# Weaving one image's way back with the next image's way forward in a spectral convolution layer

## The chip, the cores and the metric

The kernel runs on one core of a Trainium2 chip. The metric is device time in microseconds for one launch, the median of several runs. The profile is one execution, taken by the hardware profiler.

## The reference

Two layers on x of shape (4, 192, 128, 128), float32, each with a residual and a group normalisation (32 groups) ahead of it. Layer 0, the one that the change concerns, does this for each image:

```python
x1 = c1x1(gn(x), conv1_w)                      # 192 -> 48 channels
x_0, x_05, x_1 = x1[:, :16], x1[:, 16:32], x1[:, 32:48]
Fre = frft2d(x_05, 0.5)                        # fractional Fourier transform, 2-D
mag, pha = abs(Fre), angle(Fre)
mag_out = c1x1(c3x3(mag * mask1) * mask1 + c1x1(mag * mask2) * mask2)
pha_out = c1x1(pha)
ifrft = abs(frft2d(mag_out * exp(1j * pha_out), -0.5))
fre = rfft2(x_1)
mo, po = c1x1(abs(fre)), c1x1(angle(fre))
x_1o = irfft2(mo * exp(1j * po))
x = x + c1x1(concat([c1x1(x_0), ifrft, x_1o]), conv2_w)    # 48 -> 192 channels
```

Layer 1 is a selective state space scan over the 16384 positions of each image (384 inner channels, 16 states). It takes most of the time and isn't touched.

## The kernel before

Layer 0 treats the four images b = 0..3 in turn, with four kinds of work, each a Python generator. Its `yield`s mark the places at which another generator's instructions may be put in between. Program order is only the first input: the tile framework's scheduler may move an instruction ahead of others on its engine, inserts all semaphores and holds a tile's next writer until its last reader is done. Each engine, and SP's queue of DMA issues, then works through its own fixed order.

- `analysis(b)`: reads the image in 16 pieces of 8 rows (`load`, L196), takes statistics of each on DVE (`bn`, L202), finishes the group statistics (`bn_done`, L209 and L56 to L67), scales the weights of the first 1x1 convolution, and reads the pieces again (the last four, `KEEP`, are kept) for that convolution on PE (L292). ACT adds the bias (L296) and stores the result to the DRAM tensor `d1` from its own queue (L302). 33 steps: 16 pieces, then 16 pieces more, and the end.
- `branches(b)`, its first part, the way forward: reads 32 channels of d1 as `img` (L308). `spectrum` applies the two-sided transforms as matmuls with constant matrices (L224, L234), ACT and DVE copy real and imaginary part out (L240, L242), and `_polar` makes magnitude and phase: Square, Abs, Sqrt and Arctan on ACT (L76 to L90), an addition on POOL (L78), and twelve operations on DVE (L84 to L96), of which the reciprocal at L87 is the longest. This is done in three portions: two halves of the fractional branch, whose results SP stores to `dmag` and `dp` (L317), and the Fourier branch, stored to `dh` (L324).
- `branches(b)`, its second part, the way back: reads magnitude (`magQ`, L330 to L336) and phase (L353) in another layout, does the masked 3x3 convolution (L362) and the 1x1 convolutions (L254) in four steps, and `_from_polar` (L109 to L118) makes real and imaginary part, stored to `df` (L386). The Fourier branch follows in the same way from `dh` (L397) to `di` (L406). Then the inverse transforms: eight steps of L421 and L429 with ACT between, reading df (L414); four of L451 and L459, reading di (L442). The result goes to the DRAM tensor `dimg` (L467).
- `synthesis(b)`: for each of 16 pieces, reads the piece of x again (L196) and the channels of d1 and dimg into `cat` (L479, L480), does the last 1x1 convolution (L485), adds it to x on DVE (L489), takes statistics for layer 1 (L202) and stores to `xmid` from POOL's queue (L493). 16 steps and the end.

The order is written out by hand. analysis(0) runs alone. Then, for each image, branches(b) sets the beat: at each of its steps, one or two steps of analysis(b+1) and of synthesis(b-1) are taken, and what is left of these follows. For the last image, synthesis(2) starts from step `HOLD` = 10, and at step `LOADS` = 18 four pieces for synthesis(3) are read ahead. synthesis(3) runs alone.

Pools: image pieces `xt` have 7 buffers, polar temporaries `u` (128 x 1040 float32) 10, shared by the ways forward and back, `img` 2, and the temporaries of the convolutions and inverse transforms 2 each. PSUM has four single banks `ps` for all kinds of work and two double banks `pr`. Layer 1 opens its pools when those of layer 0 are closed.

Of the kernel before, what the change touches and what calls it, by code (L numbers as in the profile page):

```python
# [22 lines left out]
NC = 16  # L23
# [79 lines left out]
def _from_polar(nc, pool, half_pi, mag, pha, n):  # L103

    def tmp():
        return pool.tile([128, NC * L], F32, name="u")[:, 0:n]

    k, co = tmp(), tmp()
    nc.vector.tensor_scalar(k, pha, 1.0 / (2.0 * math.pi), ROUND, ALU.mult, ALU.add)  # L109
    nc.vector.tensor_scalar(k, k, -ROUND, None, ALU.add)  # L110
    for part in (TWO_PI_HI, TWO_PI_MID, TWO_PI_LO):
        nc.vector.scalar_tensor_tensor(pha, k, -part, pha, ALU.mult, ALU.add)
    nc.vector.tensor_scalar(pha, pha, PI_F32, -PI_F32, ALU.min, ALU.max)
    nc.scalar.activation(co, pha, AF.Abs)
    nc.scalar.activation(co, co, AF.Sin, bias=half_pi, scale=-1.0)
    nc.scalar.activation(pha, pha, AF.Sin)
    nc.vector.tensor_mul(pha, pha, mag)
    nc.vector.tensor_mul(mag, co, mag)  # L118
    return mag, pha


def layer0(tc, x, xmid, st2, w):
# [1 line left out]
    nc = tc.nc  # L124
    B = x.shape[0]
    KEEP = 4
    HOLD = 10
    LOADS = 18
    with ExitStack() as ctx:
        def pool(name, bufs, **kw):  # L130
            return ctx.enter_context(tc.tile_pool(name=name, bufs=bufs, **kw))

        cp = pool("l0c", 1)
        dram = pool("l0d", 2, space=DRAM)
        xp = pool("l0x", 7)
        sp = pool("l0s", 2)
        imp = pool("l0i", 2)
        zp = pool("l0z", 2)
        up = pool("l0u", 10)
        qp = pool("l0q", 1)  # L140
        psA = pool("l0p", 4, space=PSUM)
        psB = pool("l0r", 2, space=PSUM)
# [159 lines left out]
                        nc.scalar.dma_start(out=at[q], in_=x1[64 * q : 64 * q + 3 * NC])  # L302
                yield

        def branches(b, got):

            xT = imp.tile([128, 2 * NC, S], F32, name="img")
            nc.sync.dma_start(out=xT, in_=got["d1"][NC:, :].rearrange("c (h w) -> h c w", h=S))  # L308

            dm = dmag[b % len(dmag)]  # L310
            dp = dram.tile([NC * S, S], F32, name="dp")
            for half in range(2):
                mag, pha = yield from spectrum(
                    xT, 0, fr2[:, 0, :], fr2, S, (2 * half, 2 * half + 1)
# [3 lines left out]
                        out=by_row(dst, 8 * half, 8), in_=src.rearrange("k (c l) -> k c l", c=8)  # L318
                    )

            dh = [dram.tile([NC * S, L], F32, name=f"dh{i}") for i in range(2)]
            polar = yield from spectrum(xT, NC, rf1, rf2, L, range(4))
            for src, dst in zip(polar, dh):
                nc.sync.dma_start(  # L324
                    out=by_row(dst, 0, NC), in_=src.rearrange("k (c l) -> k c l", c=NC)
                )


            magQ = qp.tile([128, 18, S], F32, name="magQ")
            nc.sync.dma_start(  # L330
# [16 lines left out]
            dpv = dp.rearrange("(p r) l -> p (r l)", r=16)  # L347
            for half in range(2):
                n = 8 * S
                mo = up.tile([128, NC * L], F32, name="u")[:, 0:n]  # L350
                po = up.tile([128, NC * L], F32, name="u")[:, 0:n]
                ph = up.tile([128, NC * L], F32, name="u")[:, 0:n]
                nc.sync.dma_start(out=ph, in_=dpv[:, half * n : (half + 1) * n])  # L353
                for q in range(2):
                    r0 = 8 * half + 4 * q
                    at = slice(512 * q, 512 * (q + 1))
                    psf = linear(9, magQ[:, 1 + r0 : 5 + r0, :], 512)
                    pss = psA.tile([128, 512], F32, name="ps")
                    v = pss[:, 0 : 4 * WIN].rearrange("p (r l) -> p r l", r=4)
                    for tap in range(9):  # L360
                        i, j = divmod(tap, 3)
                        nc.tensor.matmul(  # L362
                            v, bd[:, tap, :], magC[:, r0 + i : r0 + i + 4, j : j + WIN],
                            start=tap == 0, stop=tap == 8,
                        )
                    f = zp.tile([128, 4, S], F32, name="f")
                    s = zp.tile([128, 4, WIN], F32, name="s")
                    nc.scalar.activation(
                        f, psf.rearrange("p (r l) -> p r l", r=4), AF.Identity, bias=bdb[:, 1:2]
                    )  # L370
                    fc = f[:, :, LO:HI]
                    rows = slice(1 + r0, 5 + r0)
                    nc.vector.tensor_tensor(fc, fc, _bc(rm[:, 1, rows], 2, WIN), ALU.mult)
                    nc.vector.scalar_tensor_tensor(
                        s, v, bdb[:, 0:1], _bc(rm[:, 0, rows], 2, WIN), ALU.add, ALU.mult
                    )
                    nc.vector.tensor_add(fc, fc, s)
                    nc.scalar.activation(
                        mo[:, at], linear(10, f, 512), AF.Identity, bias=bdb[:, 2:3]
                    )  # L380
                    nc.scalar.activation(
                        po[:, at], linear(11, ph[:, at], 512), AF.Identity, bias=bdb[:, 3:4]
                    )
                    yield
                for src, dst in zip(_from_polar(nc, up, half_pi, mo, po, n), df):
                    nc.sync.dma_start(  # L386
                        out=dst.rearrange("(p r) l -> p (r l)", r=16)[:, half * n : (half + 1) * n],
                        in_=src,
                    )
# [3 lines left out]
            di = [dram.tile([NC * S, L], F32, name=f"di{i}") for i in range(2)]  # L393
            inner = []
            for src in dh:
                t = up.tile([128, NC * L], F32, name="u")
                nc.sync.dma_start(out=t, in_=src.rearrange("(p r) l -> p (r l)", r=16))  # L397
                for q in range(4):
                    at = slice(4 * L * q, 4 * L * (q + 1))
                    nc.scalar.activation(  # L400
                        t[:, at], linear(12, t[:, at], 4 * L), AF.Identity, bias=bdb[:, 4:5]
                    )
                inner.append(t)
                yield
            for src, dst in zip(_from_polar(nc, up, half_pi, *inner, n), di):
                nc.sync.dma_start(out=dst.rearrange("(p r) l -> p (r l)", r=16), in_=src)  # L406


            img = imp.tile([128, 2 * NC, S], F32, name="img")
            for half in range(2):  # L410
                fq = [up.tile([128, NC * L], F32, name="u")[:, 0 : 8 * S] for _ in range(2)]
                fq = [t.rearrange("k (c l) -> k c l", c=8) for t in fq]
                for t, src in zip(fq, df):
                    nc.sync.dma_start(out=t, in_=by_row(src, 8 * half, 8))  # L414
                for q in range(4):
                    z = zp.tile([128, 2, 2, S], F32, name="zi")
                    ps = psA.tile([128, 512], F32, name="ps")
                    v = ps.rearrange("p (c r l) -> p c r l", c=2, r=2)
                    for cc in range(2):
                        for r in range(2):  # L420
                            nc.tensor.matmul(  # L421
                                v[:, cc], fq[r][:, 2 * q + cc, :], fi_cat[:, r], start=r == 0, stop=r == 1
                            )
                    nc.scalar.copy(z, v)
                    ps = psA.tile([128, 512], F32, name="ps")
                    v = ps.rearrange("p (c r l) -> p c r l", c=2, r=2)
                    for cc in range(2):
                        for r in range(2):
                            nc.tensor.matmul(  # L429
                                v[:, cc], z[:, cc, r, :], fi_cat[:, r], start=r == 0, stop=r == 1  # L430
                            )
                    sq = zp.tile([128, 2, 2, S], F32, name="sq")
                    nc.scalar.activation(sq, v, AF.Square)
                    c = 8 * half + 2 * q
                    nc.gpsimd.tensor_add(img[:, c : c + 2, :], sq[:, :, 0, :], sq[:, :, 1, :])
                    yield
            nc.scalar.activation(img[:, 0:NC, :], img[:, 0:NC, :], AF.Sqrt)

            hq = [up.tile([128, NC * L], F32, name="u") for _ in range(2)]
            hq = [t.rearrange("k (c l) -> k c l", c=NC) for t in hq]  # L440
            for t, src in zip(hq, di):
                nc.sync.dma_start(out=t, in_=by_row(src, 0, NC))  # L442
# [27 lines left out]
        def synthesis(b, got, early):  # L470
# [25 lines left out]
                yield  # L496
            bn_done(st, st2[:, b])

        got = [{} for _ in range(B)]
        for _ in analysis(0, got[0]):
            pass
        behind = iter(())
        for b in range(B):
            ahead = analysis(b + 1, got[b + 1]) if b + 1 < B else iter(())
            early = []
            for i, _ in enumerate(branches(b, got[b])):
                next(ahead, None)
                if b < B - 1 or i >= HOLD:  # L510
                    next(ahead if i % 2 and b < B - 1 else behind, None)
                if b == B - 1 and i == LOADS:
                    early = [load(b, p) for p in range(KEEP)]
            for rest in (behind, ahead):
                for _ in rest:
                    pass
            behind = synthesis(b, got[b], early)
        for _ in behind:
            pass

# [696 lines left out]
```

## Time and profile before

| | |
|---|---|
| median of 3 runs | 11385.26 us (11378.39 to 11391.84) |
| the profiled execution, its own time | 11385.68 us |
| its span, from the first to the last instruction | 11383.6 us |
| mean granted TensorE clock | 0.934 |
| PE, DVE, ACT, POOL busy | 92%, 92%, 82%, 86% of the span |
| bytes moved by DMA | 1481.93 MB |

PE is TensorE, PEld its weight loads, DVE VectorE, ACT ScalarE, POOL GpSimd, SP the engine that issues most DMAs. A line number such as L317 is that of the profiled kernel before. In a table of stages each row gives a stretch of the span in us from its start, the busy us of each engine with its instruction count in brackets, the granted TensorE clock, the mean busy share of the 16 DMA engines, and the GB/s that they moved. In a list of waits "SPq L317 <- ACT u L79" says that a DMA issue of line 317 on SP's queue stood until ACT had done line 79 on tile u; the numbers are the total in us, how often, and the longest. The profile spans the whole program; layer 0 is its first 1376 us.

### The profile page before, as it was taken

Reading aid. Unit: us, or ns where it says so; the run is one execution under the profiler, and the core shown is the slowest. Engines: PE = TensorE matmul, PEld = TensorE weight load, DVE = VectorE, ACT = ScalarE, POOL = GpSimd, SP = SyncE. Lnnn points to the kernel's source line nnn. Section 1 sums busy time; section 2 is a strip of 40 time slices with the busy share of each in tenths; the row PEclk is TensorE's granted clock in tenths of the full one; section 3 lists DMA queues with packets and bytes.
Section 4 is the critical chain, followed back from the end, with each engine's and each line's share of the span. In section 5 each row is a group of like instructions: output and inputs, shape, how many; then the busy total and the mean of one; then the engine's idle time right before and its main releaser. Section 6 shows DMA issues by size and latency. Waiting matters only on the chain.

```text
span 11383.6 us, 163735 instructions
## 1 busy us (share of the span) xinstructions
PE 10442.3 (92%) x54154; PEld 7012.0 (62%) x54154; DVE 10486.9 (92%) x11073; ACT 9317.9 (82%) x17507; POOL 9813.9 (86%) x4470
## 2 busy tenths in 40 slices
PE   4777799999999999999999999999999999999998
PEld 2444366666666666666666666666666666666666
DVE  6565689999999999999999999999999999999999
ACT  2323189889889889889889889889889889889887
POOL 0000099999999999999999999999999999999999
PEclk8888799999999999999999999999999999999999
DMA  7787744344344344344344344344344344344343
GB/s 197 199 222 184 206 127 119 114 128 120 113 128 121 112 128 122 111 128 123 110 128 124 109 128 125 108 128 126 107 129 126 106 130 127 105 130 128 104 130 99
DMA packets 1339287, 1481.93 MB, mean 130 GB/s; under 512 B 903281, under 2 KB 954214, under 8 KB 1337926
## 3 DMA queue, kind: packets, MB, share of 16 engines
q1 hardware_dynamic: 1317958, 1408.54, 42.6%
q0 software_dynamic: 13312, 50.34, 1.3%
q10 hardware_dynamic: 7168, 12.59, 0.3%
q8 instruction: 429, 7.03, 0.3%
q14 instruction: 420, 3.44, 0.1%
HBM read 1312.63 MB, written 155.32 MB: 129 GB/s over the span
## 4 chain that ended last, share of the span: by engine, by line
DVE 31%; ACT 29%; PE 27%; issue 8%; DMA 3%; POOL 2%; DVEq 0%; SPq 0%; POOLq 0%; ACTq 0%
DVE h L892 21%; ACT da L822 9%; ACT dbT L866 6%; PE py L918 6%; DVE op L842 5%; PE ps L686 4%; PE ps L705 4%; PE ps L956 4%; ACT L822 3%; PE op L878 2%; ACT op L822 2%; ACT L713 1%; POOL db L850 1%; PE ps L675 1%; ACT dt L770 1%
## 5 line engine op out<-in xcount | busy, mean ns | idle before, releaser
L905 POOL TENSOR_TENSOR hc<-h,bc 128x1024 f32<-128x1024 f32 x3072 | 7188.5, 2367 | 216.5 <-PE ps L942 142.2
L892 DVE TENSOR_TENSOR_SCAN h<-da,carry,op 128x512 f32<-128x512 f32 x4216 | 5197.9, 1261 | 19.6 <-ACT da L822 6.5
L918 PEld LDWEIGHTS py<-ident,hc 128*128 128x128 f32 x24576 | 2999.3, 148 | 851.2 <-issue 698.3
L918 PE MATMUL py<-ident,hc 128*128 128x128 f32 x24576 | 3401.3, 285 | 30.6 <-ACT yt L927 16.9
L822 ACT ACTIVATE da<-dt,c_A_log 128x512 f32<-128x512 f32 x4352 | 2994.7, 724 | 187.2 <-DVE h L892 172.0
L892 DVE TENSOR_TENSOR_SCAN h<-op,carry,db 128x512 f32<-128x512 f32 x1736 | 2201.1, 1268 | 128.5 <-POOL db L850 123.9
L850 POOL TENSOR_TENSOR db<-dtu,bc 128x1024 f32<-128x1024 f32 x896 | 2143.0, 2392 | 4.8 <-DMA bc<-dbc 4.7
L842 DVE TENSOR_TENSOR op<-dp,bc 128x512 f32<-128x512 f32 x2816 | 1886.6, 670 | 11.5 <-ACT dp L805 11.5
L822 ACT ACTIVATE op<-dt,c_A_log 128x512 f32<-128x512 f32 x1792 | 1223.0, 683 | 680.8 <-DVE h L892 678.0
L866 ACT ACTIVATE dbT<-ps,bT 128x128 f32<-128x128 f32 x6144 | 1656.1, 380 | 0.0
L686 PE MATMUL ps<-s,c_wiT 96*128 96x512 f32 x3072 | 1522.3, 620 | 5.2 <-ACT xs L699 3.6
L705 PE MATMUL ps<-xs,dcw 128*128 128x512 f32 x3072 | 1424.7, 593 | 1.4 <-ACT u L713 1.4
L878 PE MATMUL op<-ident,dbT 128*128 128x128 f32 x6144 | 1077.1, 296 | 112.5 <-DVE h L892 76.8
L878 PEld LDWEIGHTS op<-ident,dbT 128*128 128x128 f32 x6144 | 780.6, 151 | 408.2 <-ACT dbT L866 208.2
L686 PEld LDWEIGHTS ps<-s,c_wiT 96*128 96x128 f32 x3072 | 557.8, 199 | 469.6 <-issue 461.8
L822 ACT ACT_TABLE_LOAD x635 | 814.7, 1283 | 11.2
L705 PEld LDWEIGHTS ps<-xs,dcw 128*128 128x128 f32 x3072 | 533.6, 190 | 433.4 <-issue 431.7
L956 PE MATMUL ps<-yg,c_woT 128*96 128x512 f32 x1536 | 712.1, 600 | 79.9 <-DVE xm L962 79.9
L765 PE MATMUL ps<-xd,c_dtT 12*128 12x512 f32 x768 | 515.0, 760 | 165.0 <-DVE s L642 99.9
L493 POOL DMA_DIRECT2D xmid<-xt x64 | 41.9, 654 | 708.1 <-DVE xt L489 593.5
L956 PEld LDWEIGHTS ps<-yg,c_woT 128*96 128x96 f32 x1536 | 241.0, 163 | 447.0 <-issue 321.7
L774 POOL TENSOR_TENSOR dtu<-dt,u 128x512 f32<-128x512 f32 x384 | 478.5, 1275 | 34.5 <-ACT dt L770 34.5
(172 smaller groups left out, 10235.7 us busy)
## 6 DMA issues: line engine op xcount, KB each, us to landing
bc<-dbc SPq DMA_DIRECT2D x1024, 1024.0 KB, 5.9
xt<-in_x SPq DMA_DIRECT2D x176, 768.0 KB, 8.8
xmid<-xt POOLq DMA_DIRECT2D x64, 768.0 KB, 6.1
xm<-xmid SPq DMA_DIRECT2D x128, 384.0 KB, 3.6
carry<-h SPq DMA_DIRECT2D x3072, 1.0 KB, 1.9
out<-xm SPq DMA_DIRECT2D x128, 384.0 KB, 3.3
d<-x ACTq DMA_DIRECT2D x64, 192.0 KB, 7.0
df<-u SPq DMA_DIRECT2D x16, 512.0 KB, 5.7
```

The lines of the kernel that those rows point to most:

```text
L686: nc.tensor.matmul(pp, wiT[:, t, m * 128 : (m + 1) * 128], s[:, t, :], start=t == 0, stop=t == 1)
L705: nc.tensor.matmul(pc, dcw[:, j, k, :], xs[:, j, k : k + T], start=k == 0, stop=k == 3)
L765: nc.tensor.matmul(d[j], dtT[rows, :], xd[rows, :], start=True, stop=True)
L822: nc.scalar.activation(da, got[n]["dt"][j], AF.Exp, scale=A[:, j, st : st + 1])
L842: nc.vector.tensor_tensor(dbs[s], g["dp"], g["bc", k % NG][:, 0, q, :], ALU.mult)
L850: nc.gpsimd.tensor_tensor(db, _bc(g["dtu"][j], 1, G), g["bc", sg][:, 0], ALU.mult)
L866: nc.scalar.activation(t[:, blk, :], g["tu", j][:, blk, :], AF.Identity, scale=g["bT"][:, blk, st : st + 1],)
L878: nc.tensor.transpose(db[:, blk * 128 : (blk + 1) * 128], t[:, blk, :], ident)
L892: nc.vector.tensor_tensor_scan(h[:, q, :], das.pop(s), dbs.pop(s) if db is None else db[:, q, :], 0.0 if ch == 0 else g["before"][:, j, st ...
L905: nc.gpsimd.tensor_tensor(hc, h, g["bc", sg][:, 1], ALU.mult)
L918: nc.tensor.matmul(py[:, blk, :], hc[:, q, blk * 128 : (blk + 1) * 128], ident, start=first, stop=sg == NG - 1 and q == G - 1 and blk == T ...
L956: nc.tensor.matmul(po[0:CH], woT[:, j, t * CH : (t + 1) * CH], g["yg", j], start=j == 0, stop=j == NJ - 1,)
```

## The change

`branches` is cut in two generators: `forward` (9 steps) and `backward` (19 steps), which hand over `dp` and `dh` in the image's dictionary. A new function `weave` takes several generators with their step counts and advances all of them in proportion. Five phases replace the four turns of the loop: phase p weaves backward(p-1), forward(p), analysis(p+1) and synthesis(p-2), as far as these exist. analysis(0) stays alone at the start, synthesis(3) alone at the end; the four early reads for it now come at turn `LOADS` = 14 of the last phase. Within a turn backward's step is put first, then forward's, analysis' and synthesis'.

The pools change with it: temporaries of the way back get a pool of their own (`v`, 4 buffers), the way forward keeps `u` with 7. The phase is now read into the tile that also takes the result (`po`), in place of a tile `ph`. `f` and `sq` go from 2 buffers to 1. The DRAM pool has as many buffers as there are images, where it had 2, since dp, dh, d1 and dimg live longer. The operations themselves are the same.

```diff
-    HOLD = 10
-    LOADS = 18
+    LOADS = 14
...
-        dram = pool("l0d", 2, space=DRAM)
+        dram = pool("l0d", B, space=DRAM)
...
-        up = pool("l0u", 10)
+        up = pool("l0u", 7)
+        vp = pool("l0v", 4)
...
-        def branches(b, got):
+        def forward(b, got):
...
-            dp = dram.tile([NC * S, S], F32, name="dp")
+            dp = got["dp"] = dram.tile([NC * S, S], F32, name="dp")
...
-            dh = [dram.tile([NC * S, L], F32, name=f"dh{i}") for i in range(2)]
+            dh = got["dh"] = [dram.tile([NC * S, L], F32, name=f"dh{i}") for i in range(2)]
...
+        def backward(b, got):
+
+            dm, dp, dh = dmag[b % len(dmag)], got["dp"], got["dh"]
...
-                mo = up.tile([128, NC * L], F32, name="u")[:, 0:n]
-                po = up.tile([128, NC * L], F32, name="u")[:, 0:n]
-                ph = up.tile([128, NC * L], F32, name="u")[:, 0:n]
-                nc.sync.dma_start(out=ph, in_=dpv[:, half * n : (half + 1) * n])
+                mo = vp.tile([128, NC * L], F32, name="v")[:, 0:n]
+                po = vp.tile([128, NC * L], F32, name="v")[:, 0:n]
+                nc.sync.dma_start(out=po, in_=dpv[:, half * n : (half + 1) * n])
...
-                    f = zp.tile([128, 4, S], F32, name="f")
+                    f = zp.tile([128, 4, S], F32, name="f", bufs=1)
...
-                for src, dst in zip(_from_polar(nc, up, half_pi, mo, po, n), df):
+                for src, dst in zip(_from_polar(nc, vp, half_pi, mo, po, n), df):
...
-                    sq = zp.tile([128, 2, 2, S], F32, name="sq")
+                    sq = zp.tile([128, 2, 2, S], F32, name="sq", bufs=1)
...
+        def weave(works, early=None):
+
+            n = max(count for _, count in works)
+            for i in range(n):
+                for work, count in works:
+                    for _ in range((i + 1) * count // n - i * count // n):
+                        next(work, None)
+                if early is not None and i == LOADS:
+                    early.extend(load(B - 1, p) for p in range(KEEP))
+            for work, _ in works:
+                for _ in work:
+                    pass
...
         got = [{} for _ in range(B)]
-        for _ in analysis(0, got[0]):
-            pass
-        behind = iter(())
-        for b in range(B):
-            ahead = analysis(b + 1, got[b + 1]) if b + 1 < B else iter(())
-            early = []
-            for i, _ in enumerate(branches(b, got[b])):
-                next(ahead, None)
-                if b < B - 1 or i >= HOLD:
-                    next(ahead if i % 2 and b < B - 1 else behind, None)
-                if b == B - 1 and i == LOADS:
-                    early = [load(b, p) for p in range(KEEP)]
-            for rest in (behind, ahead):
-                for _ in rest:
-                    pass
-            behind = synthesis(b, got[b], early)
-        for _ in behind:
-            pass
+        weave([(analysis(0, got[0]), 1)])
+        early = []
+        for p in range(B + 1):
+            works = []
+            if p:
+                works.append((backward(p - 1, got[p - 1]), 19))
+            if p < B:
+                works.append((forward(p, got[p]), 9))
+            if p + 1 < B:
+                works.append((analysis(p + 1, got[p + 1]), 2 * NPIECE + 1))
+            if p >= 2:
+                works.append((synthesis(p - 2, got[p - 2], []), NPIECE + 1))
+            weave(works, early if p == B else None)
+        weave([(synthesis(B - 1, got[B - 1], early), 1)])
```

More of the change, by code (lines that the diff above doesn't have):

```diff
@@ L105, in tmp @@
     def tmp():
-        return pool.tile([128, NC * L], F32, name="u")[:, 0:n]
+        return pool.tile([128, NC * L], F32, name="v")[:, 0:n]
     k, co = tmp(), tmp()
@@ L381, in branches @@
                     nc.scalar.activation(
-                        po[:, at], linear(11, ph[:, at], 512), AF.Identity, bias=bdb[:, 3:4]
+                        po[:, at], linear(11, po[:, at], 512), AF.Identity, bias=bdb[:, 3:4]
                     )
                     yield
-                for src, dst in zip(_from_polar(nc, up, half_pi, mo, po, n), df):
+                for src, dst in zip(_from_polar(nc, vp, half_pi, mo, po, n), df):
                     nc.sync.dma_start(
@@ L395, in branches @@
             for src in dh:
-                t = up.tile([128, NC * L], F32, name="u")
+                t = vp.tile([128, NC * L], F32, name="v")
                 nc.sync.dma_start(out=t, in_=src.rearrange("(p r) l -> p (r l)", r=16))
@@ L404, in branches @@
                 yield
-            for src, dst in zip(_from_polar(nc, up, half_pi, *inner, n), di):
+            for src, dst in zip(_from_polar(nc, vp, half_pi, *inner, n), di):
                 nc.sync.dma_start(out=dst.rearrange("(p r) l -> p (r l)", r=16), in_=src)
@@ L410, in branches @@
             for half in range(2):
-                fq = [up.tile([128, NC * L], F32, name="u")[:, 0 : 8 * S] for _ in range(2)]
+                fq = [vp.tile([128, NC * L], F32, name="v")[:, 0 : 8 * S] for _ in range(2)]
                 fq = [t.rearrange("k (c l) -> k c l", c=8) for t in fq]
@@ L437, in branches @@
             nc.scalar.activation(img[:, 0:NC, :], img[:, 0:NC, :], AF.Sqrt)
-            hq = [up.tile([128, NC * L], F32, name="u") for _ in range(2)]
+            hq = [vp.tile([128, NC * L], F32, name="v") for _ in range(2)]
             hq = [t.rearrange("k (c l) -> k c l", c=NC) for t in hq]
```

## The prediction, made before the changed kernel was run

> **What bounds the kernel now.** I read the page's second part first, to find where the span is not yet full:
>
> ```profile
> span 11383.6 us, 163735 instructions
> ...
> PE   4777799999999999999999999999999999999998
> ...
> DVE  6565689999999999999999999999999999999999
> ...
> POOL 0000099999999999999999999999999999999999
> ```
>
> A digit is 284.6 us. From the sixth on, PE, DVE and POOL are all at nine tenths: that is layer 1, which the diff does not touch. In the first five DVE and PE are half idle: layer 0. Its end is the final group statistic on PE at 1376 us (POOL's first operation of layer 1, the memset of ident at 1376.32, is released by it). Layer 1's pools cannot open before layer 0's close, so every us taken from layer 0 is taken from the span, and none can come from elsewhere: 1376 us is all that is at stake.
>
> Then I cut layer 0 at its own events, seen on SP's timeline: first read of image 0's transform input (L308) at 125.5, the conv part of its way back from 205.5, its result stored (L467) at 391.0, the same stores for images 1 and 2 near 720 and 1040, the magnitude and phase of image 3 finished near 1100, its way back over near 1290. The table of stages:
>
> ```profile
> core 0: us, PE busy (x) PEld busy (x) DVE busy (x) ACT busy (x) POOL busy (x), PEclk, DMA share, GB/s
> 0.00:125.50 125.50, 37.63 (x138) 12.84 (x138) 53.21 (x93) 11.93 (x18) 0.20 (x4) 0.94 0.89 244
> 125.50:205.50 80.00, 40.53 (x192) 35.01 (x192) 64.95 (x70) 33.25 (x45) 8.19 (x3) 0.76 0.81 210
> 205.50:391.00 185.50, 142.71 (x530) 80.21 (x531) 89.86 (x124) 57.44 (x82) 5.88 (x8) 0.89 0.77 191
> 391.00:720.00 329.00, 246.54 (x862) 134.66 (x861) 203.41 (x252) 91.39 (x127) 25.75 (x28) 0.81 0.78 206
> 720.00:1040.00 320.00, 237.13 (x830) 130.11 (x829) 192.84 (x239) 91.56 (x126) 23.03 (x26) 0.81 0.81 213
> 1040.00:1100.00 60.00, 34.89 (x166) 26.12 (x164) 53.86 (x40) 30.86 (x40) 8.30 (x3) 0.81 0.31 69
> 1100.00:1290.00 190.00, 146.66 (x472) 76.27 (x474) 117.95 (x149) 41.07 (x57) 16.07 (x24) 0.81 0.75 206
> 1290.00:1376.00 86.00, 70.36 (x132) 22.63 (x128) 77.86 (x102) 0.00 (x0) 10.07 (x16) 0.50 0.84 261
> ```
>
> No engine is full in any stage. Going forward, DVE is full and PE idle (1040 to 1100: DVE 54 of 60, DMA 0.31); going back, PE leads and DVE is half idle (205 to 391: 90 of 185). One image's chain, 80 + 185.5 = 265 us, is what sets the pace; the rest is fitted around it. The first stage alone, statistics and first convolution of image 0, is the DMA's: share 0.89.
>
> The queue's own waits in layer 0 show how the chain holds the transfers:
>
> ```profile
> SPq L479 <- PE pr L485: 204.1, 51, 18.0
> ...
> SPq L317 <- ACT u L79: 75.3, 7, 20.3
> SPq L317 <- DVE u L96: 43.6, 8, 22.2
> SPq L324 <- DVE u L96: 35.4, 4, 20.5
> SPq L386 <- DVE u L117: 31.8, 6, 18.3
> ```
>
> SP is one queue in order: while it waits up to 22 us for a polar result to store, no image load behind it starts.
>
> **The Trainium skill.** "Perfetto Trace Analysis", Optimization Strategy, says that where the most-contended engine changes over time, interleaving the regimes may help. The table above is such a case. Its next paragraph says that a repeating gap can mean too few buffers; here that bears on the smaller pools of the change. "TensorE: Matmul & The Clock Gate", What's actually happening, says that the PE clock is released by recent activity: the trace agrees (granted clock 0.89 in the densest stage with transforms, 0.76 to 0.81 in the sparse ones, 0.50 in the last). "DMA: Bandwidth & Descriptors", Issuing engines are not separate DMA queues, says that all queues share the same 16 engines; so the bytes below are one sum.
>
> **The change, part by part.** Instruction counts of layer 0 don't change (the compiled order has 1657 PE and 1066 DVE rows in both); 4 of 35 activation table loads go (12 at L90 become 9, 4 at L66 become 3), 4 x 1.28 us on an ACT that is under a third busy: nothing on the path.
>
> *Loads of the four kinds of work for one image.* DMA, from the issue sizes, at 205 GB/s / 0.767 = 267 GB/s (mean rate and share of the first 1400 us): analysis 28 pieces of 0.786 MB and 3.1 MB of d1, 25.2 MB = 94 us; forward 5.3 MB = 20 us; backward 11.8 MB = 44 us; synthesis 28.3 MB = 106 us. PE, from the groups by line over four: 35, 44, 108, 57 us. DVE: 44 (64 bn_stats of 0.676 and aggregates), 61 (three polars of 19 us, of which the reciprocal at L87 is 6.5, and copies), 37, 78 us.
>
> *Stages after.* The weave gives: analysis 0; P0 = forward 0 with analysis 1; P1 = backward 0, forward 1, analysis 2; P2 = backward 1, forward 2, analysis 3, synthesis 0; P3 = backward 2, forward 3, synthesis 1; P4 = backward 3, synthesis 2; synthesis 3. The compiled SP order shows 12.6 MB (first pass of analysis 3) pulled ahead from P2 into the tail of P1, and P1 and P2 loads moved past the df, dh and di transfers, as before. I fill each stage to 0.85 of its largest load (layer 0 reached 0.96 on DMA and 0.88 on PE and 0.87 on DVE in its best 100 us, and 0.78 to 0.81 in the stages of 320 us), with PE's loads times 0.81/0.89 = 0.91 for a denser PE's clock.
>
> - Analysis 0: 125, as now.
> - P0: DMA 94 + 20 = 114; /0.85 = 134.
> - P1: DMA 94 + 20 + 44 + 47 = 205; /0.85 = 242. PE is 187, DVE 164.
> - P2: DMA 217, PE 245 x 0.91 = 223; /0.85 = 262.
> - P3: PE 209 x 0.91 = 190, DVE 176, DMA 170; 190/0.85 = 224.
> - P4: bounded by backward's chain, 190 now (1100 to 1290), plus the exposed loads below, 15: 205.
> - Synthesis 3: 86, as now.
>
> Sum 1278, against 1376: 98 us less.
>
> *Pools.* Backward gets four tiles v where it shared ten u. The second phase load (L353, now into the tile po itself) must wait for a tile that _from_polar frees, and dh loads likewise: a load of 9.0 us and one of 6.2 us, each hidden before, 15 us per image. Behind them on SP stand image loads and cat loads. In P1 to P3 forward and analysis cover this on PE and DVE; in P4 only synthesis does, so I charge it there. Bounds: 0 (synthesis covers it) and 4 x 15 = 60 us (nothing does). Forward with seven u tiles can't start a second half before the first polar is over: its matmuls have 33 turns to do so. One tile of f and of sq: the next writer comes a step (6.5 us) later than the reader (POOL's add 0.73, PE's 1.0): nothing; cover gone, at most 16 x 1 + 32 x 0.7 = 38 us. The DRAM pool moves its tensors to other addresses; no row prices that. I take 0 and, as a bound either way, the 13 us by which runs of one kernel differ (11378 to 11392).
>
> *The added stage.* One more stage is added at each end of the pipeline in exchange: P0 and P4 are partly empty, and their 134 and 205 are in the sum.
>
> **Time.** The profiled execution took 11385.68 us with a span of 11383.6; 2.1 us lie outside it, and its own time is 0.4 above the median of the runs (11385.26). 11383.6 - 98 + 2.1 = 11288.
>
> **Rivals.**
> 1. *Fuller weave.* DMA gets to 0.93 of its time in P0 to P2 and P3 is filled as well; PE stays warm: 125 + 123 + 222 + 240 + 204 + 195 + 86 = 1195, time 11205. For it: the stretch from 300 to 400 us already had DMA 0.96. Against: SP's waits for polars remain as many as they were.
> 2. *No change.* The scheduler already carried image 1's forward matmuls (L224 at 384.6) ahead of image 0's store at 391.0 and half of analysis 2's statistics into image 0's stage; if the weave only renames this and the fill stays 0.80 or less without a warmer clock, the sum is 125 + 143 + 258 + 306 + 261 + 205 + 86 = 1384: 8 us slower, within what can be told. Against: 1040 to 1100 has nothing woven in it, and now would.
> 3. *Slower: backward becomes longer, and it sets every stage.* Each engine works through its compiled order, so each of backward's three _from_polar may stand behind a forward polar of 19 us on DVE, and SP, blocked on a v tile, holds loads: 185 + 3 x 19 + 15 = 257 for P1, and with synthesis another 55 (what 320 us now takes over 265): 312 for P2 and P3. Sum 125 + 134 + 257 + 312 + 312 + 205 + 86 = 1431, time 11441. It decides where P1 + P2 + P3 exceed 826 us (I have 728). For it: the small v pool. Against: DVE's sums of 164 to 198 leave room in 242 to 262.
>
> That the change doesn't weave is excluded by the compiled order: between image 0's first two polars, where DVE had none, 16 bn_stats now stand.
>
> **Numbers.** My forecast with its fills from 0.82 to 0.9 has 0.54, rival 1 0.2, rival 2 with near variants 0.1, rival 3 and milder forms of it 0.16. About 0.2% (23 us) is what a measurement of this kernel can tell from no change. Faster by more than that 0.74, within it 0.1, slower 0.16. The range for 8 in 10 runs from 11195 (rival 1 and 10 of the 13 us for the unpriced) to 11400 (no change, and a mild form of rival 3).
>
> **What would show it.** Right: POOL's first ident memset near 1278; DMA share 0.85 from 125 to 900; no stretch like 1040 to 1100 with DMA at 0.31; PE's clock above 0.85 in P2; the wait of L317 on L79 shorter. The forecast is wrong if the middle stages last over 826 us, or if SP's waits for v tiles (L355, L399, L416) come to over 60 us with DVE and PE idle beside them; layer 1's length (10,008 us) changing would undo the whole argument.

## The result, and the profile after

The changed kernel takes 11370.17 us (median of 20 runs, 11358.66 to 11375.24); the kernel before, 11382.53 us in 20 runs of the same measurement. The ratio is 0.9987, with a 95% interval of 0.9981 to 0.9993: some 12 us faster, where the prediction had 97. The direction was right, and an eighth of the size came. Medians of the kernel before differ by up to 11 us from one round of measurements to the next (by up to 7 us on one chip), so below each kernel is compared by its ratio to the kernel before, measured on the same chip in the same round. Most intervals are 0.0015 to each side, so by estimate two kernels of different rounds are told apart from some 24 us on.

The profiled executions are 19 us apart (11385.68 and 11366.28), a little more than the medians. The first memset of `ident`, POOL's start on layer 1, is the border between the layers; the second line of the pair is that of the kernel after:

```profile
1376.32 0.20 POOL masks.py:197 MEMSET ident<- 128x128 f32 x1 [5.16 <-PE ps L63]
```

```profile
1358.24 0.20 POOL masks.py:197 MEMSET ident<- 128x128 f32 x1 [5.15 <-PE ps L63]
```

From there to the span's end it is 10,007 us before and 10,006 after. Layer 1 is untouched, and all of the difference lies in layer 0.

The page's second part of the kernel after:

```profile
span 11364.2 us, 163771 instructions
...
PE   4777799999999999999999999999999999999998
...
DVE  5666599999999999999999999999999999999999
```

PE has the same digits as before, and no digit of DVE moves by more than one: the coarse view shows no denser layer 0. The table of stages is cut at SP's first read of each image's `img` (L308: 126.1, 269.8, 516.8, 795.1), at the store of image 2's `dimg` (L469, near 1062) and, as in the prediction's table, where PE's matmuls of synthesis 3 begin (L487, near 1270). The phases P0 to P4 are rows two to six:

```profile
core 0: us, PE busy (x) PEld busy (x) DVE busy (x) ACT busy (x) POOL busy (x), PEclk, DMA share, GB/s
0.00:126.10 126.10, 37.70 (x138) 11.92 (x138) 54.73 (x96) 11.86 (x18) 0.20 (x4) 0.95 0.90 242
126.10:269.80 143.70, 84.97 (x347) 48.78 (x348) 83.10 (x110) 44.87 (x62) 7.08 (x3) 0.77 0.84 229
269.80:516.80 247.00, 181.72 (x699) 108.61 (x697) 150.09 (x178) 90.01 (x123) 14.10 (x11) 0.86 0.76 188
516.80:795.10 278.30, 215.33 (x804) 115.80 (x804) 190.75 (x230) 86.98 (x120) 24.82 (x27) 0.85 0.84 228
795.10:1062.00 266.90, 187.10 (x692) 112.23 (x692) 161.81 (x186) 78.40 (x105) 23.50 (x26) 0.81 0.64 173
1062.00:1270.00 208.00, 155.99 (x506) 79.86 (x504) 131.05 (x166) 42.88 (x60) 16.64 (x25) 0.80 0.74 206
1270.00:1356.00 86.00, 68.54 (x128) 22.17 (x128) 76.89 (x98) 0.00 (x0) 10.09 (x16) 0.50 0.85 261
```

The phases are there, and from 1040 to 1100 the DMA engines now have a share of 0.57, where it was 0.31. But a stretch with as few transfers has come up elsewhere, in P1:

```profile
350.00:410.00 60.00, 35.87 (x123) 24.76 (x124) 31.41 (x41) 19.61 (x28) 4.55 (x4) 0.76 0.28 85
```

And the fifth row, P3 (backward 2, forward 3, synthesis 1), is filled by nothing: PE 187 of 267, DVE 162, DMA 0.64. That is 43 us over its term.

What stood idle there is seen in the engines' waits in layer 0. A line says who waited, for which line's result, total us, how often, and the longest. PE's waits for loads of the way back, before:

```profile
PE ps L421 <- DMA u<-df: 14.2, 4, 10.4
PE ps L254 <- DMA u<-dh: 11.2, 3, 4.6
PE ps L254 <- DMA u<-dp: 9.1, 2, 8.0
```

and after, with the wait that grew most on DVE:

```profile
DVE u L242 <- ACT u L240: 157.0, 18, 21.0
...
PE ps L423 <- DMA v<-df: 67.5, 7, 18.9
PE ps L254 <- DMA v<-dh: 45.0, 6, 14.2
...
PE ps L254 <- DMA v<-dp: 5.4, 2, 3.9
```

PE stood 34.5 us for these loads before and 117.9 us after. By phases, P1 to P4, the waits after are 37.8, 31.3, 46.8 and 2.1 us. P3 shows one such place, on PE's timeline (start, duration, operation, and in brackets the idle time ahead of it and its releaser):

```profile
897.20 1.96 PE L487 MATMUL pr<-cat,w2x 49*96 49x512 f32 x8
918.10 1.19 PE L423 MATMUL ps<-c_fi_cat,v 128*128 128x256 f32 x2 [18.93 <-DMA v<-df]
931.41 2.93 PE L423 MATMUL ps<-c_fi_cat,v 128*128 128x256 f32 x6 [12.12 <-DMA v<-df]
```

and on SP's queue of DMA issues:

```profile
911.67 0.39 SPq L416 DMA_DIRECT2D v<-df  x1
924.56 2.09 SPq L408 DMA_DIRECT2D di<-v  x2
926.73 3.27 SPq L416 DMA_DIRECT2D v<-df  x3
```

The inverse transform needs two tiles of df. The read of the first is issued at 911.67. The others wait until the Fourier branch's result has left its tiles (L408, 924.56), because the four tiles of `v` are all taken. PE meanwhile stands at L423, and everything put behind it in its queue stands too: 31 us in one place.

### The profile page after: what moved, and what is told of

The parts are those of the page before. It is cut to its first block, busy times and chain, and to the rows that moved or that the text cites. A ratio compares the mean times of both kernels' runs of the same rounds, so it can differ in the third digit from the quotient of the medians.

```text
span 11364.2 us, 163771 instructions
## 1 busy us (share of the span) xinstructions
PE 10431.7 (92%) x54154; PEld 6995.9 (62%) x54154; DVE 10480.6 (92%) x11073; ACT 9340.5 (82%) x17503; POOL 9811.8 (86%) x4470
## 4 chain that ended last, share of the span: by engine, by line
ACT 28%; DVE 27%; PE 25%; issue 8%; POOL 3%; DMA 1%; DVEq 0%; POOLq 0%; SPq 0%; ACTq 0%
DVE h L903 18%; ACT da L833 8%; DVE op L853 6%; PE py L929 6%; ACT dbT L877 6%; PE ps L697 4%; PE ps L716 4%; PE ps L967 4%; ACT L833 3%; PE op L889 2%; POOL db L861 2%; ACT op L833 1%; ACT L724 1%; ACT dt L781 1%; PE ps L686 1%
```

## The experiments

The theories were: (a) four tiles for the way back are too few, so its reads start late; (b) another wait sets the pace: DVE's at L242, or SP's queue with the reads of cat in it; (c) the way forward itself takes P3's time, by its work or by its place in the in-order queues; and, once these were in, (d) the order within a turn, backward first. "x6v6" below is the changed kernel with 6 image pieces and 6 tiles v.

**One shared pool** (e1_shared11, against the changed kernel):

```diff
-        up = pool("l0u", 7)
-        vp = pool("l0v", 4)
+        up = pool("l0u", 11)
+        vp = up
```

The tiles `v` are also named `u` here, so that both ways take from the same eleven buffers.

> The changed kernel with one pool of 11 tiles for the ways forward and back, in place of 7 and 4; the same bytes. T1 (four tiles for the way back make its loads late: in layer 0 PE waits 118 us for them, against 35 before): these waits fall below 60 us and layer 0 ends 30 to 50 us sooner, time 11320 to 11340. T2 (the way back is long because its instructions stand among those of the next image's way forward on every engine, whatever the tiles): within 10 us of the changed kernel, 11360 to 11380.

Ratio 0.9985 [0.9978, 0.9992], the same as the changed kernel. PE's waits for df, dh and dp came to 65.6, 20.8 and 26.5 us: less for dh, more for dp. Eleven tiles in common leave the way back no better off than four of its own.

**The small pool in the old order** (e2_old_split, against the kernel before):

```diff
-        up = pool("l0u", 10)
+        up = pool("l0u", 7)
+        vp = pool("l0v", 4)
...
-                ph = up.tile([128, NC * L], F32, name="u")[:, 0:n]
-                nc.sync.dma_start(out=ph, in_=dpv[:, half * n : (half + 1) * n])
+                nc.sync.dma_start(out=po, in_=dpv[:, half * n : (half + 1) * n])
...
+                    f = zp.tile([128, 4, S], F32, name="f", bufs=1)
...
+                    sq = zp.tile([128, 2, 2, S], F32, name="sq", bufs=1)
```

> The kernel before, in its own order, with the pools of the change (7 and 4 tiles, phase read into po, one tile of f and of sq). T1: the way back gets the same late loads without a weave to cover them, 30 to 60 us slower than before, 11415 to 11445. T2: within 10 us of before, 11372 to 11392.

Ratio 1.0011 [1.0002, 1.002]: the pools of the change alone cost some 12 us in the old order. PE's waits for the loads grew from 34.5 to 82.4 us (50.4, 28.7, 3.3), so a longer wait of PE's isn't always that much more time.

**More tiles for the way back** (e3_x6v6 with its control e4_x6v4):

```diff
-        xp = pool("l0x", 7)
+        xp = pool("l0x", 6)
...
-        vp = pool("l0v", 4)
+        vp = pool("l0v", 6)      # e3; e4 stays at 4
```

> The changed kernel with 6 tiles for the way back, paid for with one of the seven image pieces (6). Read against 6 pieces and 4 tiles. T1: 30 to 50 us faster than that. T2: within 10 us of it.

> The changed kernel with 6 image pieces and 4 tiles for the way back: the control for the run with 6 and 6. Both theories: one piece less makes the transfers start later, 0 to 30 us slower than the changed kernel, 11370 to 11400.

x6v6 0.9956 [0.9941, 0.9971]; x6v4 0.9996 [0.9988, 1.0005]. In the same round on one chip the medians are 11323.01 and 11369.15: two tiles are worth 46 us, and the seventh image piece less than can be told. With six tiles the waits were

```profile
PE ps L423 <- DMA v<-df: 46.4, 7, 18.4
...
PE ps L254 <- DMA v<-dh: 33.0, 4, 13.8
```

against 73.0 and 48.9 us in x6v4. The pair differs in these two tiles alone, so it is shown that the pool costs about half of the 85 us that are missing.

**More tiles in the old order** (e5_old_x6u12: the kernel before with `l0x` 6, `l0u` 12):

> The kernel before in its own order, with 6 image pieces and a pool of 12 tiles in place of 7 and 10. If the gain of the run with 6 and 6 comes from the weave once it has tiles enough, the old order gains nothing from two more: within 15 us of before. If it is the tiles alone, whatever the order, it is 30 to 50 us faster than before.

Ratio 0.9999 [0.999, 1.0008]. The old order gains nothing from two more tiles when they are paid for with an image piece; what that piece alone is worth there wasn't tried. It is the weave that needs the tiles.

**Where the tiles come from** (e11_x6u6v7 and e12_x7u6v5: `_polar` rewritten, with results written over their operands, so that the way forward needs one tile fewer; only the first of its lines is shown):

```diff
-    ax, ay, big, pha = b, tmp(), tmp(), tmp()
+    ax, ay, pha = b, tmp(), tmp()
...
-        up = pool("l0u", 7)
-        vp = pool("l0v", 4)
+        up = pool("l0u", 6)
+        vp = pool("l0v", 7)      # e11, with l0x 6; e12: 5, with l0x 7
```

> The changed kernel with 6 pieces, and the polar rewritten to need 6 tiles u in place of 7 (maximum, mask and sign are written over their operands, the same count of operations), which leaves 7 tiles for the way back. T1: one tile more is worth less than the first two (46 us): 0 to 15 us faster than 6 and 6. If the u tiles matter to the way forward, up to 10 us slower.

> The changed kernel with 7 pieces, 6 tiles u with the rewritten polar, 5 tiles for the way back. T1: half of the gain of two tiles, 15 to 30 us faster than the changed kernel, some 11335 to 11350.

0.9946 [0.9931, 0.9961] and 0.9949 [0.9934, 0.9964]. Neither can be told from x6v6. One tile more than four already brings what two bring, more than was expected of it (with `_polar` rewritten as well, so it isn't shown for the tile alone), and a seventh adds nothing that can be seen.

**DVE's wait at L242** (e6_evac_act, against x6v6):

```diff
-                nc.vector.tensor_scalar(
-                    im[:, at].rearrange(split4, b=2, c=2), v[:, :, :, 1, :], 0.0, None, ALU.add
-                )
+                nc.scalar.copy(im[:, at].rearrange(split4, b=2, c=2), v[:, :, :, 1, :])
```

> The changed kernel with 6 pieces and 6 tiles, and the imaginary part of each spectrum group (L242) copied out by ACT, which is a third busy, in place of DVE. DVE stands 124 us at this copy in the run with 6 and 6, with additions and statistics of other images queued behind it. T2 (instructions of the two images in one queue hold each other up, the copy above all): 20 to 60 us faster than 6 and 6. T1 (the tiles were all there was): within 10 us of it.

0.9955 [0.994, 0.9969] against x6v6's 0.9956. DVE's longest wait, 157 us in the changed kernel and 124 in x6v6, is worth nothing. With the copy on ACT, DVE doesn't stand there any more, but it stands elsewhere: its waits for PE at synthesis' addition rise from 99 to 150 us, those for image pieces from 106 to 140, those at the copy to `img` (L464 in x6v6) from 35 to 64. The time is the same.

**The reads of cat off SP's queue** (e7_cat_pool, against x6v6):

```diff
-                    nc.sync.dma_start(out=cat[64 * q : 64 * q + NC, :], in_=d1[0:NC, at])
-                    nc.sync.dma_start(out=cat[64 * q + NC : 64 * q + 3 * NC, :], in_=dimg[:, at])
+                    nc.gpsimd.dma_start(out=cat[64 * q : 64 * q + NC, :], in_=d1[0:NC, at])
+                    nc.gpsimd.dma_start(out=cat[64 * q + NC : 64 * q + 3 * NC, :], in_=dimg[:, at])
```

> The changed kernel with 6 and 6, and the reads into cat issued from POOL's queue in place of SP's. On SP they stand 221 us in the changed kernel for PE to be done with cat, and everything on SP stands behind. T3 (SP's one queue is what holds the weave): 20 to 50 us faster than 6 and 6. T1 and T2: within 10 us of it, or slower, since POOL's own stores then stand behind them.

0.9985 [0.9978, 0.9992]: slower than x6v6 by some 33 us. SP's longest wait in this kernel, and POOL's for `cat`:

```profile
SPq L196 <- DMA xmid<-xt: 395.9, 50, 27.4
```

```profile
POOL cat L481 <- PE pr L487: 307.6, 50, 22.0
```

The wait of cat for its tile, 199.0 us on SP in x6v6, has only moved to POOL, where it is 307.6, and there the stores to xmid stand behind it. Image pieces then come free late: SP waits 396 us for them, 149.6 in x6v6. The Trainium skill's "DMA: Bandwidth & Descriptors", Issuing engines are not separate DMA queues, says that another issuing engine saves only issue time; here it cost time, by this reading through what stood behind the moved reads. The page lists POOL's transfers under another kind of queue (software_dynamic: 50 MB in x6v6, 63 here), and what that kind itself costs wasn't tried apart.

**Is DVE's work on the path?** (e8_norecip against x6v6, e9_old_norecip against the kernel before):

```diff
-    nc.vector.reciprocal(big, big)
-    nc.vector.tensor_mul(pha, pha, big)
+    nc.vector.tensor_scalar(pha, pha, 1.5, None, ALU.min)
```

> The changed kernel with 6 and 6, where each polar's reciprocal and multiplication (L87, L88: 7.75 us of DVE) are left out for one minimum with 1.5 (0.68 us), so that the phases are other numbers; 12 polars, 85 us of DVE less, three of them in each of four phases. T2 with DVE as the queue in which they meet: the way back no longer stands behind them, 40 to 80 us faster than 6 and 6. If DVE has room and the wait lies elsewhere: under 20 us faster.

> The kernel before, its own order and pools, with the same cut in the polar (reciprocal and multiplication left out for one minimum; the phases are other numbers). It is the control for that cut in the weave, which brought 51 us. If the cut works there because DVE is where the two images meet (T2), the old order, where forward and backward of one image follow each other, gains the plain length of the chain or less: up to 12 x 7 = 85 us if every polar lies open on the chain. If it gains much more than 51 us, the weave did hide polars, about that much of them; if about the same, the weave hid none of them; if less, polars cost the weave more than they cost the old order.

0.9907 [0.9892, 0.9922] and 0.993 [0.9913, 0.9947]. From x6v6 it takes 56 us by the ratios, from the old order 79, of 85 us of DVE work. The old order leaves nearly all of every reciprocal open on the path, and even in the weave about two thirds of it is. Whether the weave covers the rest isn't shown: the difference of the two, 23 us, is within its uncertainty of about 30.

**The way forward out of P3** (e10_no_fwd3, e13_nopolar3, against x6v6):

```diff
-            if p < B:
+            if p < B - 1:
                 works.append((forward(p, got[p]), 9))
+            if p == B - 1:
+                got[p].update(dp=got[p - 1]["dp"], dh=got[p - 1]["dh"])
```

> The changed kernel with 6 pieces and 6 tiles, with the way forward of image 3 left out of phase P3 (backward 3 then works on image 2's phases and image 1's magnitudes; image 3's result is another). P3 then holds backward 2 and synthesis 1, as P4 holds backward 3 and synthesis 2. The way forward alone took 80 us before. T2 (the chains add in the in-order queues, though nothing but the queues ties them): P3 falls from 255 to about 185, time 65 to 75 us less than 6 and 6. If the weave hides the way forward: P3 falls by under 30 us.

```diff
-            return _polar(nc, up, re, im, n)
+            return (re, im) if plain else _polar(nc, up, re, im, n)
```

> The changed kernel with 6 pieces and 6 tiles, where image 3's way forward keeps its transforms on PE and its copies, but its three polars are left out (real and imaginary part are stored as magnitude and phase; image 3's result is another). Leaving out the whole way forward in P3 brought 77 us. If it is the polars (57 us of DVE, ACT hops beside them) that the way back stands behind: 50 to 75 us faster than 6 and 6. If it is the transforms' place in PE's queue (44 us of PE, in a stage where PE is at 0.73 to 0.8): under 25 us. If both lie open in part: 25 to 50.

Without forward 3 the ratio is 0.9886 [0.9872, 0.9901], 80 us less than x6v6. Its P3, beside that of x6v6, which is shown first:

```profile
772.00:1027.00 255.00, 184.83 (x690) 111.22 (x692) 164.04 (x189) 78.28 (x105) 25.02 (x27) 0.83 0.66 183
```

```profile
770.00:950.00 180.00, 143.59 (x488) 74.26 (x486) 124.50 (x152) 43.71 (x60) 16.05 (x24) 0.86 0.79 232
```

The stage falls by 75 us (76 from one store of dimg to the next), though only 41 us of PE work and 40 of DVE work left it. Woven in, forward costs more than its own work on any engine. With image 3's transforms kept and only its polars out, the ratio is 0.9936 [0.9921, 0.9951], some 23 us less than x6v6, which is about the uncertainty of the difference; P3 falls by 11 us. So more than half of the 80 us hangs on what was kept, the transforms, the copies and the transfers, not on DVE's long polar. That speaks for theory (c) in the form "its place in the queues"; it doesn't say in which queue.

**The order within a turn** (e14_turned on x6v6, e15_turned_after on the changed kernel, e16_fwd_first on x6v6, e17_turned_x7u6v5 on e12):

```diff
-            weave(works, early if p == B else None)
+            weave(works[::-1], early if p == B else None)      # e14, e15, e17
```

```diff
+            if 0 < p < B:
+                works[0], works[1] = works[1], works[0]          # e16
```

> The changed kernel with 6 pieces and 6 tiles, where within each turn the order is synthesis, analysis, forward, backward, in place of the other way round. If the order in which the weave puts them decides how long the way back stands behind the way forward: over 20 us away from 6 and 6, in either direction. If the queues are filled as far as the chains allow: within 15 us.

> The changed kernel itself, its pools as they are (7 pieces, 7 and 4 tiles), with the order within each turn reversed and nothing else. With 6 pieces and 6 tiles the reversal brought 45 us. If the order is a cause by itself: 30 to 60 us faster than the changed kernel, about 11310 to 11340. If it needs the two tiles: under 15 us.

> The changed kernel with 6 pieces and 6 tiles, with forward put ahead of backward in each turn, and analysis and synthesis after both as before. If it is forward against backward that the reversal mended: 30 to 50 us faster than 6 and 6. If it is that backward's waits for its loads now come behind the convolutions of the other images, which fill PE meanwhile: under 20 us.

> Reversed turns with 7 pieces, 6 tiles u (rewritten polar) and 5 for the way back. The tiles brought 43 us and the reversal 45 with the tiles, so if the two add: about 11275, as the reversal with 6 and 6; if a seventh piece helps the reversed order too, up to 20 us less.

| kernel | order in a turn | tiles v | ratio [95%] | PE's waits for df, dh, dp, us |
|---|---|---|---|---|
| changed | backward first | 4 | 0.9987 [0.9981, 0.9993] | 67.5, 45.0, 5.4 |
| e15 | synthesis first, backward last | 4 | 0.9954 [0.994, 0.9969] | 56.1, 19.0, 14.7 |
| x6v6 | backward first | 6 | 0.9956 [0.9941, 0.9971] | 46.4, 33.0, 7.1 |
| e16 | forward ahead of backward | 6 | 0.9939 [0.9923, 0.9956] | 31.3, 13.0, 12.4 |
| e14 | synthesis first, backward last | 6 | **0.9911** [0.9894, 0.9928] | 13.3, 6.0, 12.2 |
| e17 | the same, 7 pieces, `_polar` rewritten | 5 | 0.9927 [0.9913, 0.9942] | 35.3, 6.5, 13.0 |

e14 has the lowest time of all kernels that do the whole computation: 11277.93 us against 11377.15 in its round, 99 us less, the size that the prediction had for the change. Turning the order alone takes 38 us off the changed kernel; more tiles alone take 35 us (the seventh piece given up for them); both together 86; each of these is uncertain by some 20 us. P3 in e14:

```profile
771.30:992.60 221.30, 183.75 (x690) 108.18 (x690) 169.68 (x192) 79.37 (x106) 27.06 (x27) 0.89 0.72 205
```

P3 has the same 690 PE instructions and 184 us of PE work as in x6v6, in 221 us in place of 255, and the granted clock goes from 0.83 to 0.89. PE's waits for the loads in P3, first x6v6, then e14:

```profile
PE ps L423 <- DMA v<-df: 18.9, 2, 18.4
PE ps L254 <- DMA v<-dh: 13.8, 1, 13.8
```

```profile
PE ps L254 <- DMA v<-dh: 0.4, 1, 0.4
```

Work that is ready stands ahead of the waiting matmuls in PE's queue, and the loads land while it runs. The reversal reorders SP's, DVE's and ACT's queues as well, and no run turns PE's alone, so this reading rests on the waits.

Both kernels reach P3 at 772 us: in the profiled executions the whole gain lies in P3, 34 us, and P4, 17 us. In P4 it is another wait. PE hardly stands for the loads there (3 us in x6v6, 4 in e14). It stands for DVE's part of the group statistics at the end of a synthesis, first x6v6, then e14:

```profile
PE ps L56 <- DVE mv L209: 18.4, 2, 13.2
```

```profile
PE ps L56 <- DVE mv L209: 4.9, 1, 4.9
```

Putting forward alone ahead (e16) gives 19 us by the ratios, but its interval overlaps that of x6v6. In its profile P3 lasts 227 us from one store of dimg to the next, where x6v6 has 255 and e14 220, so most of P3's gain seems to come from forward's place; P4, which has no forward, keeps its order in e16. How the rest divides between analysis and synthesis wasn't tried. e17 and e14 can't be told apart by their intervals.

## Why the prediction was right and wrong

Stage by stage, in us, with the same borders for all; the three columns on the right are what was measured:

| | predicted | after | x6v6 | e14 |
|---|---|---|---|---|
| analysis 0 | 125 | 126 | 124 | 128 |
| P0 | 134 | 144 | 146 | 132 |
| P1 | 242 | 247 | 238 | 234 |
| P2 | 262 | 278 | 264 | 278 |
| P3 | 224 | 267 | 255 | 221 |
| P4 | 205 | 208 | 201 | 184 |
| synthesis 3 | 86 | 86 | 89 | 89 |

- **What bounds it: right.** Only layer 0 moved. The first stage, the last one and the instruction counts came as said, and P2's clock is 0.85, just at the mark that was set. Two readings of the page were loose: in the first five slices PE stands mostly at seven tenths, which is not half idle, and DVE reaches nine tenths in the seventh slice. The sum doesn't use them.
- **P3, the step that failed.** Its load came out: PE 187 us measured, 190 predicted, in part by luck (next point). Its fill did not: 0.85 was assumed, 0.70 came. That is 43 of the 78 us missing from the sum (1278 predicted, 1356 measured). I took the fill from the best 100 us of the old order; in its stages of 329 and 320 us PE had only 0.75 and 0.74. In P3 the three works share one PE queue in a fixed order, and PE stood 46.8 us for backward's loads. In e14 the same stage has a fill of 0.83 and takes 221 us.
- **The factor 0.91 for a denser PE's clock: not confirmed.** P3's clock stayed at 0.81, so the 190 held because the 209 it was made from was too high. PE's busy time for P3's 690 or so instructions is 187, 185 and 184 us in the changed kernel, x6v6 and e14, at clocks of 0.81, 0.83 and 0.89. Nor does the granted clock simply follow PE's busy share, as the prediction read it from the skill and the trace: in its own table the first stage has 0.94 with PE busy 38 of 125 us, and the last 0.50 with 70 of 86.
- **"In P1 to P3 forward and analysis cover this": wrong.** This is the pools' term. I charged 15 us, in P4 alone. It was the other way round: of PE's 118 us of waits for these loads, 83 more than before, P4 had 2 and P1 to P3 the other 116; P3 had 47 of them, and it has no analysis to cover anything. Two more tiles took 46 us off the time. Forward doesn't cover a wait of PE's when its matmuls stand behind the waiting one. The Trainium skill's "Perfetto Trace Analysis", Optimization Strategy, says that repeating gaps can mean too few buffers; here they did in part, and the runs give the size.
- **The order within a turn: taken as free, and wasn't.** No step of mine priced that backward's step comes first and synthesis' last. It costs 38 us with four tiles and about 51 with six, by the ratios.
- **P2 and P0: the loads were short, the fill was right.** P2's DMA came to 0.84 x 278 = 234 us where I had 217 (and PE 223 as the largest); 234/0.85 = 275. Much of analysis 3's first pass, which I had put in P1, ran in P2: SP issued 33 image reads in P1 and 39 in P2, where the forecast has 44 and 28. P0's DMA was 121 us, not 114. Together 26 us. P1's term held only because both errors cancelled there: its DMA was 188 us, not 205, at a fill of 0.76.
- **P4: right in its number**, 208 for 205, but not by its parts. The 15 us of exposed loads came as 2 us of PE's waits. The 190 that I took for backward's bare chain is no floor: with the turns reversed the stage takes 184.
- **Rival 3** named the true mechanism, backward stretched by what is woven into the in-order queues. It put it on DVE, behind the polars. DVE's wait for ACT (157 us) looked the part, and e6 showed it to be worth nothing; e10 and e13 put most of forward's cost in P3 on what is left without the polars. But the polars aren't free in the weave: the reciprocals alone are worth 56 us over the four images (e8). P1 + P2 + P3 came to 792 us, short of the 826 at which the change would have been slower.
- **Rival 1**, a fuller weave, did not come: DMA's share in P0 to P2 is 0.84, 0.76 and 0.84, not 0.93.
- **Rival 2**, that the old order already had the overlap, is refuted by e14: the same operations go in 99 us less. What it gave as the time, near no change, was nearly what was measured, for another reason.
- **What would show it.** Of the signs of being right, L317's wait on L79 did fall (75.3 to 57.9 us), but DMA's share in P1 and P3 is 0.76 and 0.64, not 0.85, and a stretch with a share under 0.31 is there. As a sign of being wrong I had named SP's waits for v tiles, over 60 us. On SP's list L399, L355 and L416 for v show only 11.7, 10.2, and 8.7 and 8.5 us. The cost stood on PE's list instead, as waits for the loads themselves.
- **Left open:** the DRAM pool's other addresses were not tried alone.

So the 97 us were there, though e14 finds them in other stages than the forecast: P2 is 16 us longer than predicted and P4 21 us shorter. About half was lost to the tiles of the way back, about half to the order within a turn; each was tried alone and together with the other.

## What to carry to other kernels

When several independent works are woven into in-order queues, a sum of loads by engine says how short a stage could be, not how short it will be: ask of each turn which instruction can wait and what ready work stands behind it, and try the work of the longest dependency chain last in the turn, as it paid here. A stage that holds two images' chains at once needs buffers for both. Before a long wait in the list is believed, take it away: DVE's longest here (157 us) was worth nothing, while several shorter ones on PE decided.

## What the runs showed of the hardware

After PE had stood 14 us for dh, eight matmuls 128x260 of L254 took 3.68 us; eleven us later the next eight of that line took 2.02:

```profile
883.87 3.68 PE L254 MATMUL ps<-v,c_bd 128*128 128x260 f32 x8 [14.20 <-DMA v<-dh]
...
895.25 2.02 PE L254 MATMUL ps<-v,c_bd 128*128 128x260 f32 x8
```

So a wait on PE can cost more than its own length: the matmuls behind it ran slower too. It agrees with the Trainium skill's "TensorE: Matmul & The Clock Gate", What's actually happening, by which recent activity releases PE's clock, and with P3's granted clock, 0.81 in the changed kernel and 0.89 in e14. In all it is little: PE's busy time in P3 differs by 3 us between the two. And moving reads to another issuing queue was not neutral: it lengthened SP's waits for the stores to xmid from 150 to 396 us.
